# A macaron layer's setup: the FFN weight quantised on VectorE alone in a written order, the projection's weight and the attention bias prepared later, the second stack of values loaded three slots sooner

## The chip, the cores and the metric

The kernel runs on one core of one Trainium2 chip. The metric is the device time of one execution in microseconds, as the median of several runs. A profile of one execution shows what each engine did: TensorE (PE, and PEld for its weight loads), VectorE (DVE), ScalarE (ACT), GpSimd (POOL), and SyncE (SP), which issues nearly all DMAs.

## The reference

Input x is (4, 4096, 512) in float32: 16384 tokens of 512 features. The layer is half a feed-forward, a neighbourhood attention (16 heads of 32, 13 keys around each query, a relative bias per head), and the same half feed-forward again, each with a layer norm and a residual. The feed-forward quantises both its input and its weight in blocks of 32 to a 6-bit float grid.

```python
def _mx_quantize(t, eps=1e-30):
    blocks = t.reshape(rows, K // BLOCK_SIZE, BLOCK_SIZE)
    scales = jnp.maximum(jnp.max(jnp.abs(blocks), axis=-1) / FP6_E2M3_MAX, eps)
    q = _nearest_on_grid(blocks / scales[..., None], _GRID)
    return (q, scales)

def _L0_ffn_ref(x, weight, bias):
    xq, xs = _mx_quantize(x2);  wq, ws = _mx_quantize(w2)
    return (xq * xs[..., None]) @ (wq * ws[..., None]).T + bias

def _L0_attn_ref(x, qkv_w, qkv_b, rpb, proj_w, proj_b):
    qkv = x @ qkv_w.T + qkv_b
    attn = jnp.einsum('bhld,bhlkd->bhlk', q * SCALE, k[:, :, nbr, :]) + rpb[:, bidx][None]
    attn = jax.nn.softmax(attn, axis=-1)
    out = jnp.einsum('bhlk,bhlkd->bhld', attn, v[:, :, nbr, :])
    return out @ proj_w.T + proj_b

x = x + 0.5 * _L0_ffn_ref(_layernorm(x), ffn_weight, ffn_bias)
x = x + _L0_attn_ref(_layernorm(x), qkv_w, qkv_b, rpb, proj_w, proj_b)
x = x + 0.5 * _L0_ffn_ref(_layernorm(x), ffn_weight, ffn_bias)
```

## The kernel before

Every large product is made of float16 pairs: each operand is split into a high and a low half, and `product` (L146–154) runs 3 × 4 matmuls of 128 × 128 by 128 × 512. The halves are made by a ScalarE copy (`high`) and a VectorE subtraction followed by a DMA transpose on SyncE's queue (`low`). All five weight matrices lie transposed in one tile `wt`: query, key, value, projection (16 row chunks, numbered 0–3, 4–7, 8–11, 12–15) and FFN (16–19).

The work on the 128 token tiles is a pipeline written out by hand in slots. `begin(slot, stage, rank)` puts a generator into a slot, each `yield n, rank` moves its rest n slots on, and `run_slot` issues a slot's stages by rank. A tile t advances 7 slots behind tile t−1 (`STEP`). For a tile: load at 7t−18, moments (bn_stats) and the quantised norm from 7t−11 on (eight stages: factors on GpSimd, yq on ScalarE, block maxima on VectorE, a GpSimd product by 1/scale, the 8-bit rounding on ScalarE, a GpSimd product by the scale, high on ScalarE, low with the xT transpose), first feed-forward product (`pmf`) at 7t+5, second norm with the hln transpose at 7t+11, value product (`pmv`) at 7t+20. Four tiles form a group. For each of its four items of four heads (item m at 7m): Q/K products (`pmqk`) at +38, scores and softmax from +42 with the pT transpose at +52, the product with the values (`pv`) at +59. Output product (`pmo`) at 7t+93 and second feed-forward at 7t+105 end a tile.

The values go through DRAM (`vd`). `load_stack` (L394) reads them back as overlapping windows of keys, two stacks a group (head pairs 0–1 of items, and 2–3), three DMAs of about 357 KB each. The two stacks share a pool of two buffers (`vsp`). They are loaded at slots 28n+46 and 28n+56 for group n (L618–619).

The setup, from L622 on: the FFN weight `fw`, small inputs, tiles 0–2 and 16 row chunks `rows` are loaded. `junk` (L651) sums the squares of all rows on ScalarE; `powers` (L663) turns the largest into powers of two `up` and `down` by way of two small TensorE products. The FFN weight is then quantised in four chunks (L738–763): on VectorE the division, subtractions of `u`, a second division, the addition and the rounding to the grid (`tie_to_lower`); on GpSimd the two products `u` (L748) and the product back (L759); on ScalarE the 8-bit cast and the high half. Tiles 1 and 2 are normalised, and `scales`, `put_scaled` (high on ScalarE, low on VectorE, transpose into `wt`), `attention_bias` (the value bias taken through the projection, 12 matmuls `pmb`) and `put_table` (the relative bias, from the DMAs `rd`, `shifted`, `masks`) stand in slots 0 to 35.

What sets the order: up to `tc.manual_schedule()` at L772 the framework's scheduler orders the instructions of each engine by its own cost model; behind it, each engine runs them in the order in which the program issues them. So in this kernel the FFN weight, the first three norms and the DMAs ahead of L772 are ordered by the scheduler, and slots from −17 on as written.

```python
        begin(0, one(scales), 9)
        for slot, o in zip((2, 4, 5, 6, 10, 13, 16, 19, 21, 23, 25, 27, 29, 31, 33, 35), chunks):
            begin(slot, put_scaled(o), 9)
        begin(28, attention_bias(), 9)
```

Of the kernel before, what the change touches and what calls it, by code (L numbers as in the profile page):

```python
# [26 lines left out]
F32 = mybir.dt.float32  # L27
# [10 lines left out]
P = 128  # L38
# [26 lines left out]
def macaron_kernel(  # L65
# [96 lines left out]
    def begin(slot, stage, rank=5):  # L162
        slots.setdefault(slot, []).append((rank, stage))
# [402 lines left out]
    def one(f, *args):  # L566
        f(*args)
        return
        yield
# [45 lines left out]
    for n in range(n_batch * NG):  # L615
        k = n * GROUP * STEP
        b, g = divmod(n, NG)
        begin(k + 6 * STEP + 4, one(load_stack, b, g, 0), 9)  # L618
        begin(k + 8 * STEP, one(load_stack, b, g, 1), 9)


    with tc.tile_pool(name="setup", bufs=1) as sp, tc.tile_pool(name="scratch", bufs=2) as scr:  # L622
# [8 lines left out]
        nc.gpsimd.memset(rp, 0.0)  # L631
        nc.scalar.dma_start(out=rp[:, QR - 1 : QR - 1 + NREL], in_=rpb)


        rows = {}

        sq = sp.tile([P, 5 * KC], F32, name="sq")
        first = min(slots)
        for slot in range(first, first + EARLY * STEP, STEP):
            run_slot(slot)  # L640
        for _ in quantised_norms(-10):
            pass
        chunks = (8, 9, 10, 11, 12, 13, 14, 15, 0, 4, 1, 5, 2, 6, 3, 7)
        for o in chunks:
# [3 lines left out]
        for o in (*range(4 * KC, 5 * KC), *chunks):  # L648
# [3 lines left out]
        ptb = ps_m.tile([P, 512], F32, tag="mm", name="ptb")  # L652
        nc.tensor.transpose(ptb[:, : 3 * KC], b12, ident[: 3 * KC, : 3 * KC])
        bT = sp.tile([P, 3 * KC], F32, name="bT")
        nc.vector.tensor_copy(bT, ptb[:, : 3 * KC])
        b2 = sp.tile([P, 3 * KC], F32, name="b2")
        nc.vector.scalar_tensor_tensor(b2, bT, 2.0 ** -8, bT, ALU.mult, ALU.mult)
        nc.vector.tensor_tensor(sq[:, : 3 * KC], sq[:, : 3 * KC], b2, ALU.add)
        top5 = sp.tile([P, 5], F32, name="top5")
        up = sp.tile([P, 5], F32, name="up")  # L660
        down = sp.tile([P, 5], F32, name="down")

        def powers(lo, hi):  # L663

            w = hi - lo
            nc.vector.tensor_reduce(
                top5[:, lo:hi], sq[:, lo * KC : hi * KC].rearrange("p (m c) -> p m c", c=KC),
                AX.X, ALU.max,
            )
            ptn = ps_m.tile([P, 512], F32, tag="mm", name=f"ptn{lo}")  # L670
            nc.tensor.transpose(ptn[:w, :P], top5[:, lo:hi], ident)
            most = sp.tile([w, 1], F32, name=f"most{lo}")
# [3 lines left out]
            ones_w = sp.tile([w, P], F32, name=f"ones{lo}")  # L676
            nc.gpsimd.memset(ones_w, 1.0)
            pb = ps_m.tile([P, 512], F32, tag="mm", name=f"pb{lo}")
            nc.tensor.matmul(pb[:, :w], ones_w, diag, start=True, stop=True)
            e = sp.tile([P, w], I32, name=f"e{lo}")  # L680
# [11 lines left out]
        powers(4, 5)  # L692
        nc.vector.tensor_scalar(cf, down[:, 4:5], 0.5 / XS, None, ALU.mult)
        nc.gpsimd.tensor_scalar(half_ffn_b, half_ffn_b, 0.5, None, ALU.mult)

        def put_weights(o, hl):
            return nc.sync.dma_start_transpose(
# [19 lines left out]
        for o in range(KC):  # L717
            nc.vector.tensor_reduce(
                w_abs[:, o * NB : (o + 1) * NB], blocks(fw[:, o, :]), AX.X, ALU.max,
                apply_absolute_value=True,  # L720
            )
        nc.vector.tensor_scalar(w_sc, w_abs, 1.0 / Q_MAX, None, ALU.mult)
        split_scale()
        nc.vector.scalar_tensor_tensor(w_abs, w_hi, -Q_MAX, w_abs, ALU.mult, ALU.add)
        nc.vector.scalar_tensor_tensor(w_abs, w_lo, -Q_MAX, w_abs, ALU.mult, ALU.add)
        nc.vector.scalar_tensor_tensor(w_sc, w_abs, 1.0 / Q_MAX, w_sc, ALU.mult, ALU.add)
        nc.vector.tensor_scalar(w_sc, w_sc, Q_EPS, None, ALU.max)
        nc.vector.reciprocal(w_r, w_sc)
        split_scale()
        w_back = small("w_back")  # L730
        nc.vector.tensor_scalar(w_back, w_sc, up[:, 4:5], F8_SCALE, ALU.mult, ALU.mult)

        def large(name, o, dt=F32):
            return scr.tile(
                [P, NB, QB], dt, tag=name, bufs=3 if name == "wu_" else KC, name=f"{name}{o}"
            )

        for o in range(KC):  # L738
# [5 lines left out]
            qh, q0 = large("wqh_", o, F16), large("wq0_", o)  # L744
            nc.vector.tensor_tensor(qh, fwb, per(w_r), ALU.mult)
            for i, b in enumerate((w_hi, w_lo)):
                u = large("wu_", f"{o}_{i}")
                nc.gpsimd.tensor_tensor(u, qh, per(b), ALU.mult)  # L748
                nc.vector.tensor_tensor(fwb, fwb, u, ALU.subtract)  # L749
            nc.vector.tensor_tensor(q0, fwb, per(w_r), ALU.mult)  # L750
            nc.vector.tensor_tensor(q0, q0, qh, ALU.add)
# [12 lines left out]

        for t in range(1, EARLY):
            moments(t * STEP - 10, t, "n1")
            for _ in quantised_norms(t * STEP - 10):
                pass
# [14 lines left out]

        su, sd = up, down
        tab = sp.tile([P, 1], F32, name="tab")
        vb = sp.tile([P, KC], F32, name="vb")
# [18 lines left out]

        def attention_bias():

            vbx = sp.tile([P, 2, KC, P], F16, name="vbx")
            nc.scalar.copy(vbx[:, 0], bc(vb, P))
            nc.vector.tensor_tensor(vbx[:, 1], bc(vb, P), vbx[:, 0], ALU.subtract)  # L810
            yield 3, 9
# [100 lines left out]
```

## Time and profile before

| | |
|---|---|
| median of 3 runs | 2408.76 us (2407.12 to 2414.85) |
| the profiled execution's own time | 2401.24 us |
| its span, first to last instruction | 2399.4 us |
| granted TensorE clock, mean | 0.993 |
| TensorE / VectorE / GpSimd / ScalarE busy | 95% / 84% / 83% / 55% |
| DMA engines, SyncE's queue, share of time | 75.6% |
| first feed-forward product on TensorE | 58.72 us |
| first Q/K product | 106.72 us |

A line of a group or of the timeline reads: start and length in us, engine (a trailing q is its instruction queue, which issues DMAs), source line, operation, out<-in by the program's names, shapes and count, and in brackets how long the engine had been idle and what released it. A line of waits reads: who waited for whom, us in total, times, longest. A line of windows reads: stretch, its length, busy time of PE, PEld, DVE, ACT and POOL with counts, the granted clock, the DMA engines' share and GB/s.

### The profile page before, as it was taken

What the parts mean: (1) busy time and instruction counts of PE and PEld (TensorE: products, weight loads), DVE (VectorE), ACT (ScalarE), POOL (GpSimd) and SP (SyncE); (2) the same over time, 40 slices, a digit from 0 to 9 for tenths busy, and PEclk for the clock granted to TensorE, in tenths of its full rate; (3) what the DMA queues carried; (4) which work ended last, traced back from release to release, by engine and by line L of the source; (5) the groups of instructions that cost most, each with busy time, mean ns of one, the idle gap of its engine ahead of it and who ended that gap; (6) DMA issues with size and microseconds to landing.
All of it is one profiled execution on the core that took longest, in us unless ns stands there. A gap on an engine that the chain in (4) does not pass through costs nothing.

```text
span 2399.4 us, 82333 instructions
## 1 busy us (share of the span) xinstructions
PE 2278.8 (95%) x35539; PEld 1114.0 (46%) x35539; DVE 2015.3 (84%) x3588; ACT 1327.1 (55%) x2080; POOL 1989.0 (83%) x2012
## 2 busy tenths in 40 slices
PE   0799999999999999999999999999999999999987
PEld 0244444444444444444444444444444444444442
DVE  8789888888888888888888888888888888888775
ACT  4455555555555556555555555555555555555442
POOL 5578888888888888888888888888888888888677
PEclk9899999999999999999999999999999999999998
DMA  5788888787787877778867778777778887777753
GB/s 153 145 150 153 158 164 158 148 157 151 145 161 156 152 150 159 146 153 162 161 145 156 150 146 167 153 154 147 159 139 156 158 158 146 162 148 143 137 115 90
DMA packets 925700, 360.58 MB, mean 150 GB/s; under 512 B 718876, under 2 KB 889752, under 8 KB 925336
## 3 DMA queue, kind: packets, MB, share of 16 engines
q1 hardware_dynamic: 924992, 354.79, 75.6%
q8 instruction: 278, 4.55, 0.8%
q10 hardware_dynamic: 344, 0.53, 0.1%
q14 instruction: 86, 0.70, 0.1%
HBM read 110.15 MB, written 67.29 MB: 74 GB/s over the span
## 4 chain that ended last, share of the span: by engine, by line
PE 89%; DVE 4%; DMA 3%; issue 1%; POOL 1%; ACT 1%; SPq 0%; DVEq 0%; ACTq 0%; POOLq 0%
PE pmqk L151 27%; PE pmf L151 26%; PE pmo L151 14%; PE pmv L151 13%; PE ps L433 6%; PE pv L503 3%; DMA xT<-hlq 2%; DVE hlq L204 0%; DVE fw L749 0%; DMA x<-hln 0%; DVE qk L373 0%; DVE stn L180 0%; POOL x L564 0%; ACT ring L530 0%; DVE whl L779 0%
## 5 line engine op out<-in xcount | busy, mean ns | idle before, releaser
L151 PE MATMUL pmf<-wt,xT 128*128 128x512 f16 x3048 | 703.1, 381 | 17.8 <-DMA xT<-hlq 17.7
L151 PE MATMUL pmqk<-x,wt 128*128 128x512 f16 x3072 | 707.7, 380 | 6.2 <-DMA x<-hln 5.4
L151 PEld LDWEIGHTS <-xT 128*128 128x128 f16 x3048 | 297.0, 98 | 386.1 <-DMA xT<-hlq 29.3
L151 PEld LDWEIGHTS <-wt 128*128 128x128 f16 x3072 | 290.0, 98 | 343.1 <-issue 9.7
L151 PE MATMUL pmv<-wt,x 128*128 128x512 f16 x1536 | 353.8, 380 | 5.1 <-DMA x<-hln 5.1
L151 PE MATMUL pmo<-wt,ring 128*128 128x512 f16 x1536 | 355.3, 381 | 2.6 <-issue 2.6
L246 POOL TENSOR_TENSOR yq<-yq,r 128x1024 f32<-128x1024 f32 (+1 forms) x141 | 246.2, 1746 | 130.8 <-DVE r L244 130.8
L564 POOL TENSOR_TENSOR x<-x,half_ffn_b 128x512 f32<-128x512 f32 x256 | 327.4, 1279 | 0.1
L275 DVE SCALAR_TENSOR_TENSOR x<-pmf,coef,x 128x512 f32<-128x512 f32 x256 | 179.5, 701 | 165.2 <-PE pmf L151 164.7
L530 ACT ACTIVATE ring<-pv 128x510 f16<-128x510 f32 (+8 forms) x224 | 82.3, 414 | 400.5 <-PE pv L503 400.5
L310 ACT CAST vt<-pmv 128x512 f16<-128x512 f32 x128 | 74.9, 585 | 389.3 <-PE pmv L151 389.3
L180 DVE BATCH_NORM_STATS2 stn<-x 128x6 f32<-128x512 f32 x384 | 265.3, 691 | 8.9 <-DMA x<-in_L_attn_x_dram 0.2
L251 POOL TENSOR_TENSOR yq<-q,sc 128x1024 f32<-128x1024 fp8e4 (+1 forms) x141 | 246.7, 1749 | 0.4 <-ACT q L249 0.4
L151 PEld LDWEIGHTS <-x 128*128 128x128 f16 x1536 | 150.5, 98 | 187.6 <-DMA x<-hln 5.6
L373 DVE SCALAR_TENSOR_TENSOR qk<-pmqk,qk_b,qk 128x512 f16<-128x512 f32 x256 | 190.6, 744 | 53.8 <-ACT qk L369 53.0
L476 POOL TENSOR_TENSOR sf<-sf,total 128x714 f32<-128x714 f32 (+2 forms) x128 | 178.6, 1395 | 44.2 <-DVE total L474 25.0
L151 PEld LDWEIGHTS <-ring 128*128 128x128 f16 x1536 | 140.2, 98 | 161.5 <-issue 4.2
L186 POOL TENSOR_SCALAR rsq<-mv 128x2 f32<-128x2 f32 (+1 forms) x141 | 131.3, 931 | 96.0 <-DVE mv L181 93.8
L249 ACT ACTIVATE q<-yq,nudge 128x1024 fp8e4<-128x1024 f32 (+1 forms) x141 | 149.9, 1063 | 108.0 <-POOL yq L246 99.8
L369 ACT ACTIVATE qk<-pmqk,qk_b 128x512 f16<-128x512 f32 x256 | 176.1, 688 | 53.2 <-PE pmqk L151 52.1
L233 ACT ACTIVATE yq<-x,nbq,rsq 128x512 f32<-128x512 f32 x254 | 193.0, 804 | 20.8 <-POOL nbq L192 20.2
L467 POOL TENSOR_TENSOR sf<-sf,top 128x714 f32<-128x714 f32 (+2 forms) x128 | 180.4, 1409 | 20.0 <-DVE top L465 19.8
(145 smaller groups left out, 3466.9 us busy)
## 6 DMA issues: line engine op xcount, KB each, us to landing
vs<-vd SPq DMA_DIRECT2D x144, 357.0 KB
x<-in_L_attn_x_dram SPq DMA_DIRECT2D x128, 256.0 KB
vd<-vt SPq DMA_DIRECT2D x128, 256.0 KB
out_dram<-x SPq DMA_DIRECT2D x128, 256.0 KB
vs<-vd SPq DMA_DIRECT2D x24, 378.0 KB
vs<-vd SPq DMA_DIRECT2D x24, 315.0 KB
rows<-in_L_attn_qkv_w_dram SPq DMA_DIRECT2D x12, 256.0 KB
xT<-hlq SPq DMA_TRANSPOSE x141
```

What stands on the lines that cost most here:

```text
L151: nc.tensor.matmul(pm, lhs(a, c), rhs(b, c), start=(n == 0), stop=(n == 3 * KC - 1))
L180: nc.vector.bn_stats(st, xs[t])
L233: nc.scalar.activation(y[:, u], xs[t], AF.Identity, bias=nb[:, u : u + 1], scale=rs[:, u : u + 1])
L246: nc.gpsimd.tensor_tensor(yb, yb, bc(r, QB), ALU.mult)
L249: nc.scalar.activation(q8, y, AF.Identity, bias=nudge, saturate=False)
L251: nc.gpsimd.tensor_tensor(yb, q8.rearrange("p u (n q) -> p (u n) q", q=QB), bc(sc, QB), ALU.mult)
L275: nc.vector.scalar_tensor_tensor(xs[t], pm, cf, xs[t], ALU.mult, ALU.add)
L369: nc.scalar.activation(t[:, s, 0, KN:], pms[s], AF.Identity, bias=bias)
L373: nc.vector.scalar_tensor_tensor(t[:, s, 1, KN:], pms[s], bias, t[:, s, 0, KN:], ALU.add, ALU.subtract)
L467: nc.gpsimd.tensor_tensor(s, s, bc(top[:, :n], KN), ALU.subtract)
L476: nc.gpsimd.tensor_tensor(s, s, bc(total[:, :n], KN), ALU.mult)
L564: nc.gpsimd.tensor_tensor(xs[t], xs[t], b, ALU.add)
```

## The change

`manual_schedule` moves up to just behind the first loads, so that nearly the whole setup runs in the order in which it is written. The quantisation of an FFN chunk becomes a generator `quantise` with two yields, whose three GpSimd products run on VectorE; its steps are interleaved by hand with those of the first three norms and with the squares of the row chunks in fours. `half_ffn_b` is halved on ScalarE in place of GpSimd. `powers` and `scales` are cut into parts of one slot each. The squares now come in the order value, query and key, projection, with the projection's four last of all.

The projection's four chunks are squared early, dropped, loaded a second time at slots 61, 64, 68 and 71, and scaled five slots later, with their halves in tiles of the pool of x. The attention bias goes from slot 28 to 80. The query and key chunks take slots 13 to 35, the value chunks 3 to 6. The second stack of a group is loaded at 28n+53 in place of 28n+56.

```diff
-        begin(k + 8 * STEP, one(load_stack, b, g, 1), 9)
+        begin(k + 7 * STEP + 4, one(load_stack, b, g, 1), 9)
...
+        ctx.enter_context(tc.manual_schedule())
...
-        chunks = (8, 9, 10, 11, 12, 13, 14, 15, 0, 4, 1, 5, 2, 6, 3, 7)
+        chunks = (8, 9, 10, 11, 0, 4, 1, 5, 2, 6, 3, 7, 12, 13, 14, 15)
...
-        nc.gpsimd.tensor_scalar(half_ffn_b, half_ffn_b, 0.5, None, ALU.mult)
+        nc.scalar.activation(half_ffn_b, half_ffn_b, AF.Copy, scale=0.5)
...
+        ffn_power = powers(4, 5)
+        next(ffn_power)
...
+        next(ffn_power)
+        next(norms[0])
...
+        next(norms[0])
+        for _ in ffn_power:
+            pass
...
+        def quantise(o):
...
-            for i, b in enumerate((w_hi, w_lo)):
-                u = large("wu_", f"{o}_{i}")
-                nc.gpsimd.tensor_tensor(u, qh, per(b), ALU.mult)
+            for b in (w_hi, w_lo):
+                nc.vector.tensor_tensor(u, qh, per(b), ALU.mult)
                 nc.vector.tensor_tensor(fwb, fwb, u, ALU.subtract)
...
-            nc.gpsimd.tensor_tensor(fwb, w8, per(w_back), ALU.mult)
+            yield
+            nc.vector.tensor_tensor(fwb, w8, per(w_back), ALU.mult)
             hl = scr.tile([P, 2, dim], F16, tag="whl", bufs=4, name=f"whlf{o}")
             nc.scalar.copy(hl[:, 0, :], fw[:, o, :])
+            yield
             nc.vector.tensor_tensor(hl[:, 1, :], fw[:, o, :], hl[:, 0, :], ALU.subtract)
             put_weights(4 * KC + o, hl)
...
-        ctx.enter_context(tc.manual_schedule())
...
+        step(ready[3])
+        step(ready[2])
+        step(norms[1])
+        step(norms[2])
+        step(ready[3])
+        step(norms[1])
+        step(ready[3])
+        for _ in range(5):
+            step(norms[2])
+        for o in chunks[12:]:
+            square(o)
...
         def put_scaled(o):
             s = up[:, o // KC : o // KC + 1]
-            hl = scr.tile([P, 2, dim], F16, tag="whl", bufs=4, name=f"whl{o}")
+            if o < 3 * KC:
+                hl = scr.tile([P, 2, dim], F16, tag="whl", bufs=4, name=f"whl{o}")
+            else:
+                load_rows(o)
+                hl = xp.tile([P, dim], F32, tag="x", name=f"whl{o}").bitcast(F16)
+                hl = hl.rearrange("p (s k) -> p s k", s=2)
+                yield 5, 9
             nc.scalar.activation(hl[:, 0, :], rows[o], AF.Copy, scale=s)
...
-            powers(0, 4)
+            yield from powers(0, 4)
...
-        begin(0, one(scales), 9)
-        for slot, o in zip((2, 4, 5, 6, 10, 13, 16, 19, 21, 23, 25, 27, 29, 31, 33, 35), chunks):
+        begin(0, scales(), 9)
+        for slot, o in zip((3, 4, 5, 6, 13, 16, 20, 23, 26, 29, 32, 35, 61, 64, 68, 71), chunks):
             begin(slot, put_scaled(o), 9)
-        begin(28, attention_bias(), 9)
+        begin(80, attention_bias(), 9)
```

More of the change, by code (lines that the diff above doesn't have):

```diff
@@ L632, in macaron_kernel, with load_rows @@
         nc.scalar.dma_start(out=rp[:, QR - 1 : QR - 1 + NREL], in_=rpb)
+        ctx.enter_context(tc.manual_schedule())
         rows = {}
         sq = sp.tile([P, 5 * KC], F32, name="sq")
[L638 to L642, printed above, removed]
-        chunks = (8, 9, 10, 11, 12, 13, 14, 15, 0, 4, 1, 5, 2, 6, 3, 7)
-        for o in chunks:
+        chunks = (8, 9, 10, 11, 0, 4, 1, 5, 2, 6, 3, 7, 12, 13, 14, 15)
+        def load_rows(o):
             w, i = (qkv_w, o) if o < 3 * KC else (proj_w, o - 3 * KC)
@@ L647, in macaron_kernel, with square @@
             nc.sync.dma_start(out=rows[o], in_=w[i * P : (i + 1) * P, :])
-        for o in (*range(4 * KC, 5 * KC), *chunks):
+        def square(o):
             src = fw[:, o - 4 * KC, :] if o >= 4 * KC else rows[o]
@@ L651, in macaron_kernel @@
             nc.scalar.activation(junk, src, AF.Square, accum_out=sq[:, o : o + 1])
[L652 to L658, printed above, removed]
+        for o in range(4 * KC, 5 * KC):
+            square(o)
         top5 = sp.tile([P, 5], F32, name="top5")
-        up = sp.tile([P, 5], F32, name="up")
-        down = sp.tile([P, 5], F32, name="down")
+        up = const.tile([P, 5], F32, name="up")
+        down = const.tile([P, 5], F32, name="down")
         def powers(lo, hi):
@@ L671, in powers @@
             nc.tensor.transpose(ptn[:w, :P], top5[:, lo:hi], ident)
+            ones_w = sp.tile([w, P], F32, name=f"ones{lo}")
+            nc.gpsimd.memset(ones_w, 1.0)
+            yield 1, 9
             most = sp.tile([w, 1], F32, name=f"most{lo}")
@@ L675, in powers @@
             nc.vector.tensor_scalar(diag, ident[:w, :w], most, 2.0, ALU.mult, ALU.mult)
-            ones_w = sp.tile([w, P], F32, name=f"ones{lo}")
-            nc.gpsimd.memset(ones_w, 1.0)
             pb = ps_m.tile([P, 512], F32, tag="mm", name=f"pb{lo}")
             nc.tensor.matmul(pb[:, :w], ones_w, diag, start=True, stop=True)
+            yield 1, 9
             e = sp.tile([P, w], I32, name=f"e{lo}")
@@ L690, in powers @@
             nc.vector.tensor_scalar(d, d, 23, None, ALU.logical_shift_left)
-        powers(4, 5)
-        nc.vector.tensor_scalar(cf, down[:, 4:5], 0.5 / XS, None, ALU.mult)
-        nc.gpsimd.tensor_scalar(half_ffn_b, half_ffn_b, 0.5, None, ALU.mult)
         def put_weights(o, hl):
@@ L721, in macaron_kernel @@
             )
+        first = min(slots)
+        for slot in range(first, first + EARLY * STEP, STEP):
+            run_slot(slot)
+        for o in chunks:
+            load_rows(o)
+        ffn_power = powers(4, 5)
+        next(ffn_power)
+        nc.scalar.activation(half_ffn_b, half_ffn_b, AF.Copy, scale=0.5)
+        norms = {t: quantised_norms(t * STEP - 10) for t in range(EARLY)}
+        next(norms[0])
         nc.vector.tensor_scalar(w_sc, w_abs, 1.0 / Q_MAX, None, ALU.mult)
         split_scale()
+        next(ffn_power)
+        next(norms[0])
         nc.vector.scalar_tensor_tensor(w_abs, w_hi, -Q_MAX, w_abs, ALU.mult, ALU.add)
@@ L729, in macaron_kernel @@
         split_scale()
+        next(norms[0])
+        for _ in ffn_power:
+            pass
         w_back = small("w_back")
         nc.vector.tensor_scalar(w_back, w_sc, up[:, 4:5], F8_SCALE, ALU.mult, ALU.mult)
+        nc.vector.tensor_scalar(cf, down[:, 4:5], 0.5 / XS, None, ALU.mult)
         def large(name, o, dt=F32):
[L734 to L738, printed above, removed]
+            return scr.tile([P, NB, QB], dt, tag=name, name=f"{name}{o}")
+        def quantise(o):
             fwb = blocks(fw[:, o, :])
@@ L742, in per @@
                 return bc(t[:, o * NB : (o + 1) * NB], QB)
-            qh, q0 = large("wqh_", o, F16), large("wq0_", o)
+            qh, q0, u = large("wqh_", o, F16), large("wq0_", o), large("wu_", o)
             nc.vector.tensor_tensor(qh, fwb, per(w_r), ALU.mult)
-            for i, b in enumerate((w_hi, w_lo)):
-                u = large("wu_", f"{o}_{i}")
-                nc.gpsimd.tensor_tensor(u, qh, per(b), ALU.mult)
+            for b in (w_hi, w_lo):
+                nc.vector.tensor_tensor(u, qh, per(b), ALU.mult)
                 nc.vector.tensor_tensor(fwb, fwb, u, ALU.subtract)
@@ L758, in macaron_kernel @@
             )
-            nc.gpsimd.tensor_tensor(fwb, w8, per(w_back), ALU.mult)
+            yield
+            nc.vector.tensor_tensor(fwb, w8, per(w_back), ALU.mult)
             hl = scr.tile([P, 2, dim], F16, tag="whl", bufs=4, name=f"whlf{o}")
             nc.scalar.copy(hl[:, 0, :], fw[:, o, :])
+            yield
             nc.vector.tensor_tensor(hl[:, 1, :], fw[:, o, :], hl[:, 0, :], ALU.subtract)
             put_weights(4 * KC + o, hl)
[L765 to L768, printed above, removed]
@@ L772, in macaron_kernel, with step @@
-        ctx.enter_context(tc.manual_schedule())
+        ready = [quantise(o) for o in range(KC)]
+        def step(g):
+            next(g, None)
+        step(ready[0])
+        step(norms[0])
+        step(norms[0])
+        for o in chunks[:4]:
+            square(o)
+        moments(STEP - 10, 1, "n1")
+        step(ready[0])
+        step(norms[0])
+        step(ready[1])
+        step(ready[0])
+        step(norms[0])
+        step(norms[1])
+        step(norms[1])
+        moments(2 * STEP - 10, 2, "n1")
@@ new lines, in macaron_kernel @@
+        step(ready[1])
+        step(norms[0])
+        for o in chunks[4:8]:
+            square(o)
+        step(ready[2])
+        step(ready[1])
+        step(norms[1])
+        step(norms[1])
+        step(norms[1])
+        step(norms[2])
+        step(norms[2])
+        step(ready[2])
+        step(norms[1])
+        for o in chunks[8:12]:
+            square(o)
+        step(ready[3])
+        step(ready[2])
+        step(norms[1])
+        step(norms[2])
+        step(ready[3])
+        step(norms[1])
@@ new lines, in macaron_kernel @@
+        step(ready[3])
+        for _ in range(5):
+            step(norms[2])
+        for o in chunks[12:]:
+            square(o)
+        ptb = ps_m.tile([P, 512], F32, tag="mm", name="ptb")
+        nc.tensor.transpose(ptb[:, : 3 * KC], b12, ident[: 3 * KC, : 3 * KC])
+        bT = sp.tile([P, 3 * KC], F32, name="bT")
+        nc.vector.tensor_copy(bT, ptb[:, : 3 * KC])
+        b2 = sp.tile([P, 3 * KC], F32, name="b2")
+        nc.vector.scalar_tensor_tensor(b2, bT, 2.0 ** -8, bT, ALU.mult, ALU.mult)
@@ L774, in put_scaled @@
+        nc.vector.tensor_tensor(sq[:, : 3 * KC], sq[:, : 3 * KC], b2, ALU.add)
         def put_scaled(o):
             s = up[:, o // KC : o // KC + 1]
-            hl = scr.tile([P, 2, dim], F16, tag="whl", bufs=4, name=f"whl{o}")
+            if o < 3 * KC:
+                hl = scr.tile([P, 2, dim], F16, tag="whl", bufs=4, name=f"whl{o}")
+            else:
+                load_rows(o)
+                hl = xp.tile([P, dim], F32, tag="x", name=f"whl{o}").bitcast(F16)
+                hl = hl.rearrange("p (s k) -> p s k", s=2)
+                yield 5, 9
@@ L785, in macaron_kernel @@
         tab = sp.tile([P, 1], F32, name="tab")
-        vb = sp.tile([P, KC], F32, name="vb")
+        vb = const.tile([P, KC], F32, name="vb")
         def scales():
-            powers(0, 4)
+            yield from powers(0, 4)
             nc.vector.tensor_scalar(cp, sd[:, 2:3], sd[:, 3:4], 1.0 / XS, ALU.mult, ALU.mult)
@@ L806, in attention_bias @@
         def attention_bias():
-            vbx = sp.tile([P, 2, KC, P], F16, name="vbx")
+            vbx = xp.tile([P, dim], F32, tag="x", name="vbx").bitcast(F16)
+            vbx = vbx.rearrange("p (s c q) -> p s c q", s=2, c=KC)
             nc.scalar.copy(vbx[:, 0], bc(vb, P))
```

## The prediction

> **What bounds the kernel now.** I read the page first, then TensorE's waits, the busy time by windows, and the timeline of the start and of two DMA stretches. Page and windows:
>
> ```profile
> span 2399.4 us, 82333 instructions
> PE 2278.8 (95%) x35539; PEld 1114.0 (46%) x35539; DVE 2015.3 (84%) x3588; ACT 1327.1 (55%) x2080; POOL 1989.0 (83%) x2012
> ...
> 20.00:40.00 20.00, 0.38 (x1) 0.08 (x1) 20.00 (x31) 7.25 (x20) 15.81 (x13) 1.00 0.20 59
> ...
> 80.00:100.00 20.00, 11.78 (x37) 4.29 (x38) 18.23 (x34) 10.84 (x17) 10.08 (x16) 0.67 0.83 168
> ...
> 300.00:400.00 100.00, 100.00 (x1510) 48.97 (x1508) 87.07 (x154) 57.47 (x90) 86.86 (x85) 1.00 0.83 161
> ```
>
> A window row gives TensorE, its weight loads, VectorE, ScalarE and GpSimd, then clock, DMA share and GB/s. From about 107 us on TensorE is the bound (100 of 100 us). Of its 121 us idle, 73 lie before 107 us and some 18 in the waits of the tail after 2330. In the start VectorE is the bound: full at 20–40, 18.23 of 20 at 80–100. Only three things can win time: the start, waits of TensorE in the middle, and the tail, which the change leaves alone.
>
> The start, from the timeline: the weight products of GpSimd and VectorE in alternation, the first feed-forward product, the attention-bias product, the first Q/K product.
>
> ```profile
> 28.09 1.49 POOL L748 TENSOR_TENSOR wu<-wqh,w_lo 128x512 f32<-128x512 f16 x1
> 28.60 1.53 DVE L751 TENSOR_TENSOR wq<-wq,wqh 128x512 f32<-128x512 f32 x1
> 29.55 1.49 POOL L748 TENSOR_TENSOR wu<-wqh,w_hi 128x512 f32<-128x512 f16 x1
> 30.05 1.53 DVE L750 TENSOR_TENSOR wq<-fw,w_r 128x512 f32<-128x512 f32 x1
> ...
> 58.72 4.79 PE L151 MATMUL pmf<-wt,xT-10_160 128*128 128x512 f16 x12 [15.19 <-DMA wt<-whlf]
> ...
> 96.28 3.59 PE L151 MATMUL pmb<-wt,vbx 128*128 128x512 f16 x8 [3.67 <-DVE vbx L810]
> ...
> 106.72 5.34 PE L151 MATMUL pmqk<-x,wt 128*128 128x512 f16 x24 [1.33 <-DMA x<-hln]
> ```
>
> Each pair of one GpSimd and one VectorE product advances 1.45 us (28.60 to 30.05). Without GpSimd VectorE starts one every 0.60 (45.28, 45.88, 46.48 in the chain). So one GpSimd product costs VectorE 0.85 us.
>
> TensorE's waits between 300 and 2300 us, and the DMA queue around 480 and 146 us:
>
> ```profile
> PE pmf L151 <- DMA xT<-hlq: 7.1, 9, 1.6
> ...
> 473.69 1.58 SPq L409 DMA_DIRECT2D vs<-vd  x3
> 475.36 2.10 SPq L555 DMA_DIRECT2D out_dram<-x  x1
> 477.51 0.43 SPq L176 DMA_DIRECT2D x<-in_L_attn_x_dram  x1
> 479.02 5.29 SPq L485 DMA_TRANSPOSE pT<-p  x1
> 484.40 3.12 SPq L205 DMA_TRANSPOSE xT<-hlq  x1
> ...
> 142.26 3.73 SPq L409 DMA_DIRECT2D vs<-vd  x6
> 146.61 5.78 SPq L485 DMA_TRANSPOSE pT<-p  x1
> 153.83 1.30 SPq L205 DMA_TRANSPOSE x<-hln  x1
> 158.15 4.44 PE L151 MATMUL pmqk<-x,wt 128*128 128x512 f16 x12 [4.11 <-DMA x<-hln]
> ```
>
> The second stack load goes out just ahead of the pT transpose; pT then holds SyncE's queue 5.29 us (2.4 behind a first load, at 532.12), and xT behind it is late. The nine waits recur at one phase of the 70 us group.
>
> **The change, part by part.**
>
> *FFN weight on VectorE alone.* Before, four chunks take 8 VectorE operations each (0.60 apiece, the bit-or 0.34: 4.54, so 18.2 us), with norms, scales and small work about 25 us, and 18 GpSimd products of chunks and norms cost 18 × 0.85 = 15.3. That gives 40.5 from 15.4, so 55.9; the trace has the last VectorE step of the weight end at 55.0, so the account holds. After: 11 operations a chunk (6.34 × 4 = 25.4), two statistics 1.55, two block maxima 1.7, two low halves 1.2, and only five norm products of GpSimd in the way (4.3): 34.2 us. The e, up and down operations of the FFN power now stand ahead, so it begins at about 16.7 instead of 15.4, and ends at 50.9. [...] The new VectorE form, a product out of 8-bit values, has no row; the 0.60 of the other forms and GpSimd's contended 1.45 bound it: 0 to 3.4 us for four. I take 0.60, since GpSimd itself needs 1.04 for that form and 1.05 for float.
>
> *What is late next.* The xT transposes share one hlq buffer, so the third tile's high half waits for the second's transpose: issued about 50.4, 3.25 to land (as 55.38 to 58.63), so 53.7. Only behind that do ScalarE's last four squares run (4 × 0.62, to 57), then the maximum, transpose, diagonal and spread of the other powers (2.4 us; the FFN's took 3.0, 9.47 to 12.51, with other VectorE work between). These two small products stand ahead of the first feed-forward product on TensorE, which thus starts at 59.4 although its weights landed at about 55: 0.7 us late, bounds −4 and +4.
>
> *SyncE in the start.* The table's DMAs (rd, then shifted, masks; issue 0.68 + 1.77 + 2.45) and x3's load lay at 17.9–28.8; they now stand behind xT of tile 2 (about 55.2) and ahead of V's four transposes (1.29 each). shifted waits for rd: 6.0 us from issue in a full queue (17.86 to 23.89), 3.2 for a transpose in a free one; I take 3.2, the queue being free at 50–54 (share 0). So: xT issued by 56.5, rd landed 59.7, shifted and masks out by 64, x3 by 64.5, 3 to land (3.9 in a full queue, 5.91 to 9.81). x3 lands near 67.5 and its statistics start at 67.5 instead of 66.34: +1.2 (0 to +4). GpSimd's six mask selects (1.37) fall in its idle time; half_ffn_b's 1.51 on GpSimd becomes one ScalarE copy (0.7) beside idle time.
>
> *Projection's parts and bias out of slots 10–35.* Ahead of the fourth hln, which starts the first Q/K product, three VectorE low parts of 0.74 and vbx 0.68 go (2.9 us; 3.5 with one 1.24 contended), ScalarE loses the same number, SyncE 3 × 1.29. I take 3.5 (0 to 7: VectorE is full at 80–100, latency-bound before). TensorE's pmb leaves its 4.6 at half clock, off the path but for 0.2. First Q/K product: +1.2 − 3.5 = **−2.3 us** (−7 to +4).
>
> *The same, late.* Slots 61–77: four 256 KB loads again, four ScalarE parts (0.72), four VectorE (0.74), four transposes; vbx and after_b 0.62 + 0.68 + 0.74. At 160–180 us VectorE is busy 14.67 of 20 and the DMA share 0.55: they fit; at 180–200 VectorE has 18.55 and DMA 1.01. **+0.5** (0 to 4). pmb on the bound engine, 12 matmuls at 0.216: **+2.6**.
>
> *Second stack three slots sooner.* It now follows xT and hln, as the first load does (517.58, 519.58, 521.52). Its buffer's last reader is the pv product one slot earlier, which TensorE ends about 4 us before SyncE gets there (499.5 against 503.8): no wait. The DMA engines are idle at 470–474, so the load uses that and pT finds a freer queue; xT was at most 1.6 us late and gains about 3. **−7.1** (0 to −7.1). In the early case the DMA share at 142–146 is 0.43 and 0.56, about 2 us idle; the 4.11 wait falls by **−2** (0 to −4.1). The matmuls after it run 4.44 instead of 2.70, with a granted clock of 0.57 in 158–162; behind waits of 2.13 and 2.41 (1740, 2313) matmuls stay at full pace, so **−1.7** (0 to −1.7). [...]
>
> Sum: −2.3 + 0.5 + 2.6 − 7.1 − 2.0 − 1.7 = **−10.0 us**. The profiled execution took 2401.24 us (span 2399.4), so 2391.2; the median of the runs shown, 2408.76, lies 7.5 above it, so **2398.8**.
>
> **Rivals.**
>
> *The start wins its four microseconds too.* If the squares and the power chain run before the last norm, the first product starts at about 55: 4.4 less, **2394**. For it: TensorE has nothing else there. Against: one ScalarE queue in written order. Chance 0.15.
>
> *The stack load only moves its collision.* xT stays late by as much: without the −7.1 the sum is −2.9, **2406**. For it: DMA shares of 1.0–1.2 around both loads. Against: no xT wait follows a first load. Chance 0.22.
>
> *Slower: two loads in consecutive steps.* The first goes out at slot 46 and the second now at 53, seven slots apart instead of ten; a step with a load fills about 17 of 17.6 us of DMA (share near 1 from 516 to 532 and 534 to 540). If the backlog adds up, the xT after it is late in nearly all 30 groups; at the mean of the present waits, 0.78 us, that costs 23: −2.9 + 23, **2429**. It decides from a third of a microsecond a group. Against: behind a first load xT goes out at 535.16, needs 5.2 (484.40 to 489.61), and its product starts at 542.38, 2 us to spare. Chance 0.15.
>
> **How the numbers follow.** Forecast 0.48, rivals 0.15, 0.22, 0.15. About 0.3% (7.2 us) is what a measurement of this kernel can tell from no change. The forecast's own range, from the bounds of the start above all, is 2391 to 2405, some three quarters of it below 2401.5; with the first rival: faster 0.52. Within: a fifth of the forecast and most of the second rival, 0.32. Slower: the third rival and a sliver, 0.16. The range 2387 to 2413 leaves out most of the third rival and the far end of the start.
>
> **What would show it.** First feed-forward product at 59 ± 3 with weights landed earlier; the powers' small products just ahead of it; the first Q/K product near 104; pmb about 2.6 us long at full clock in the steady part; no xT waits between 300 and 2300, pT after second loads near 2.5–3 us; the wait before the fifth Q/K item about 2. Wrong it would be if xT waits recur elsewhere in the group, if VectorE's start ends after 55, or if Q/K start past 110.

## The result, and the profile after

The changed kernel takes 2441.35 us (median of 6 runs, 2438.58 to 2451.1); the kernel before, run beside it, 2410.43 us (6 runs, 2407.12 to 2418.08). The ratio is 1.0125, 95% interval 1.0110 to 1.0141: it is slower by about 31 us, where 10 us less had been forecast. The profiled execution took 2439.54 us.

The page of the changed kernel (busy time by engine, the granted clock in 40 slices, SyncE's DMA queue and TensorE's instruction queue, one group of instructions):

```profile
span 2437.8 us, 82350 instructions
...
PE 2290.6 (94%) x35539; PEld 1117.7 (46%) x35539; DVE 2013.5 (83%) x3600; ACT 1330.1 (55%) x2081; POOL 1976.9 (81%) x1999
...
PEclk9899999999999999999999999999999999999998
...
q1 hardware_dynamic: 925568, 355.84, 78.5%
q8 instruction: 278, 4.55, 0.8%
...
L151 PE MATMUL pmo<-wt,ring 128*128 128x512 f16 x1536 | 362.6, 386 | 18.4 <-issue 18.3
```

TensorE does the same 35539 matmuls in a span 38.4 us longer. VectorE and GpSimd have no more work than before. But the packets of SyncE's queue take 78.5% of the DMA engines' time, against 75.6% of a shorter span, for 0.3% more bytes (354.79 to 355.84 MB), and the output product now stands idle 18.3 us, named "issue": time in which the engine waited for nothing that the profile shows.

The steady window of the prediction again (length, busy PE, PEld, DVE, ACT, POOL, clock, DMA share, GB/s), and one behind a late restart:

```profile
300.00:400.00 100.00, 100.00 (x1575) 49.13 (x1573) 85.89 (x153) 58.61 (x91) 87.02 (x85) 1.00 0.81 155
1995.00:2007.00 12.00, 7.24 (x96) 3.10 (x95) 6.40 (x10) 2.28 (x5) 5.67 (x5) 0.86 0.73 131
```

The quiet 100 us are as full as before. The loss sits in single places such as the last row: TensorE works 7.24 of 12 us, at a clock of 0.86.

The start, by the timeline: three VectorE products in a row on the way to the weight (each reads what the one before wrote or writes over what it read), the powers' small products and the first feed-forward product, the attention-bias product, the first Q/K product.

```profile
16.39 0.69 DVE L755 TENSOR_TENSOR wu<-wqh,w_hi 128x512 f32<-128x512 f16 x1
17.12 0.69 DVE L756 TENSOR_TENSOR fw<-fw,wu 128x512 f32<-128x512 f32 x1
17.84 0.69 DVE L755 TENSOR_TENSOR wu<-wqh,w_lo 128x512 f32<-128x512 f16 x1
...
59.19 0.38 PE L666 MATMUL ptn<-ident,top 128*4 128x128 f32 x1 [47.11 <-DVE top L661]
60.28 0.56 PE L675 MATMUL pb<-diag,ones 4*128 4x4 f32 x2 [0.71 <-DVE diag L673]
60.77 4.50 PE L151 MATMUL pmf<-wt,xT-10_308 128*128 128x512 f16 x12
...
106.39 6.00 PE L151 MATMUL pmqk<-x,wt 128*128 128x512 f16 x14 [5.35 <-DMA x<-hln]
...
199.89 2.75 PE L151 MATMUL pmb<-wt,vbx 128*128 128x512 f16 x12 [0.74 <-DVE stn L180]
```

The first Q/K product begins 0.3 us earlier than before, but behind a wait of 5.35 us and at half clock (the trace grants 0.50 from 105.27 to 112.10): its first 14 matmuls alone take 6.00 us where 24 took 5.34. The start ends about 2.5 us later than before.

TensorE's waits between 300 and 2300 us (who waited for whom, us in total, times, longest): the issue waits of the kernel before, then all of the changed kernel, then SyncE's queue around 480 us and one of the new waits:

```profile
PE ps L433 <- issue: 3.1, 3, 1.5
PE pmo L151 <- issue: 2.6, 2, 2.1
PE pv L503 <- issue: 1.3, 3, 0.7
PE pmqk L151 <- issue: 0.8, 2, 0.5
```

```profile
PE pmo L151 <- issue: 9.2, 3, 4.8
PE ps L433 <- issue: 8.8, 6, 3.0
PE pmqk L151 <- issue: 4.8, 4, 2.5
PE pv L503 <- issue: 3.9, 7, 1.3
PE pmqk L151 <- DVE mv L181: 3.0, 1, 3.0
```

```profile
480.46 1.64 SPq L409 DMA_DIRECT2D vs<-vd  x3
...
490.46 3.12 SPq L485 DMA_TRANSPOSE pT<-p  x1
493.67 3.00 SPq L205 DMA_TRANSPOSE xT<-hlq  x1
...
1987.89 1.66 SPq L409 DMA_DIRECT2D vs<-vd  x3
1997.74 3.44 SPq L485 DMA_TRANSPOSE pT<-p  x1
...
1994.29 0.82 PE L151 MATMUL pmo<-wt,ring 128*128 128x512 f16 x3
1999.87 3.67 PE L151 MATMUL pmo<-wt,ring 128*128 128x512 f16 x9 [4.76 <-issue]
```

The waits for xT (7.1 us before) are gone, and pT behind a second load takes 3.12 us in place of 5.29, close to the forecast of 2.5 to 3. In their place "issue" waits have grown from 7.8 us in this stretch to 26.7. In the last two lines TensorE stops in the middle of one product, three matmuls in, with nine to go whose operands are the same tiles. The packet records of the trace show what arrives there. Queue q8 above, named "instruction", moved 278 blocks of 16 KB, 4.55 MB in all; by division that is 64 bytes for each of some 71 thousand matmuls and weight loads, and the blocks are taken here for TensorE's program. One of them ran from 1996.49 to 1998.38; TensorE went on 1.5 us later. The issue waits look alike from 300 us on: a 16 KB packet ends 1.2 to 1.8 us before the restart, and a stack load `vs<-vd` was issued 7 to 13 us before it. So the block of instructions is late. That it is queued behind the load's packets is the reading that the experiments put to the test.

Behind six of these waits, of 2.98 to 4.76 us, the trace grants a clock of 0.50 for 3.41 us each. The two shortest of the six are 2.98 us (before 616.11) and 3.01 (before 1781.25). A wait of 2.46 us at 1764.9 was not followed by it. In the experiments below one of 1.97 us was (late load, clock 0.57 from 1446 to 1450) and one of 3.26 us was not (sooner load alone, 1.00 from 1965 to 1974), so the length of a wait alone does not decide it in these traces.

The 38.4 us of the two spans then read: late instruction blocks +29.8 (13.8 to 43.6 us over the whole span, the 3.0 us that the profile puts down to VectorE's `mv` among them, since that wait too ends behind such a packet), half clock behind six of them +10.2 (6 × 1.7, half of 3.41 each), xT −7.1, the attention-bias product with its wait +3.3, the start +2.5, one wait at 221 +1.4, the two waits for pT in the tail −2.2: 37.9.

### The profile page after: what moved, and what is told of

Same layout as the page of the kernel before. It is cut to its first block, busy times and chain, and to the rows that moved or that the text cites. A ratio compares the mean times of both kernels' runs of the same rounds, so it can differ in the third digit from the quotient of the medians.

```text
span 2437.8 us, 82350 instructions
## 1 busy us (share of the span) xinstructions
PE 2290.6 (94%) x35539; PEld 1117.7 (46%) x35539; DVE 2013.5 (83%) x3600; ACT 1330.1 (55%) x2081; POOL 1976.9 (81%) x1999
## 3 DMA queue, kind: packets, MB, share of 16 engines
q1 hardware_dynamic: 925568, 355.84, 78.5%
q8 instruction: 278, 4.55, 0.8%
## 4 chain that ended last, share of the span: by engine, by line
PE 89%; DVE 5%; issue 2%; DMA 2%; POOL 1%; ACT 1%; SPq 0%; ACTq 0%; DVEq 0%; POOLq 0%
PE pmqk L151 27%; PE pmf L151 26%; PE pmo L151 13%; PE pmv L151 13%; PE ps L433 6%; PE pv L503 3%; DMA x<-hln 1%; DVE stn L180 1%; DMA xT<-hlq 1%; DVE hlq L204 1%; POOL x L564 0%; DVE sc L239 0%; POOL yq L246 0%; DVE wu L755 0%; DVE fw L756 0%
## 5 line engine op out<-in xcount | busy, mean ns | idle before, releaser
L151 PE MATMUL pmf<-wt,xT 128*128 128x512 f16 x3048 | 704.0, 381 | 11.5 <-DMA xT<-hlq 11.4
L151 PE MATMUL pmo<-wt,ring 128*128 128x512 f16 x1536 | 362.6, 386 | 18.4 <-issue 18.3
L373 DVE SCALAR_TENSOR_TENSOR qk<-pmqk,qk_b,qk 128x512 f16<-128x512 f32 x256 | 190.7, 745 | 73.9 <-ACT qk L369 73.4
```

The costliest lines, as they stand in the source:

```text
L151: nc.tensor.matmul(pm, lhs(a, c), rhs(b, c), start=(n == 0), stop=(n == 3 * KC - 1))
L373: nc.vector.scalar_tensor_tensor(t[:, s, 1, KN:], pms[s], bias, t[:, s, 0, KN:], ALU.add, ALU.subtract)
```

## The experiments

**First four: is it the sooner load, the start, or the burst?** Theory A had the sooner load make the instruction blocks late; rival B blamed the start and the late parts.

*The changed kernel with the second load at its old place.*

```diff
-        begin(k + 7 * STEP + 4, one(load_stack, b, g, 1), 9)
+        begin(k + 8 * STEP, one(load_stack, b, g, 1), 9)
```

> The changed kernel with the second stack put back to slot 28n+56; all else as changed. Theory A (the earlier load makes TensorE's instruction blocks arrive late: in the trace of the changed kernel the waits that end about 1.3 us after a block's packet sum to 43 us against 14 before, and the half-clock stretches behind the long ones cost 10 more): about 2441 - 30 - 10 + 7 (the xT waits return) + 2 = 2410, 2405 to 2420. Rival B (projection parts and bias late, or the new start, do the harm; the load only saved 7): 2445 to 2450.

Measured: 2466.61 us, ratio to before 1.0242 (1.0216 to 1.0268). Its waits, 300 to 2300 us:

```profile
PE pmf L151 <- DMA xT<-hlq: 20.3, 17, 2.6
PE pv L503 <- issue: 13.7, 9, 3.7
PE pmqk L151 <- issue: 9.2, 6, 2.9
PE pmo L151 <- issue: 5.8, 2, 3.0
PE ps L433 <- issue: 1.7, 1, 1.7
```

Without the sooner load it is 25 us slower still: the load is a gain in the changed kernel too. And xT waits 20.3 us in place of 7.1, though load and xT stand in the slots of before. The issue waits, 30.4 us in all, are no fewer than the 26.7 with the sooner load. Theory A falls; rival B's 2445 to 2450 was too low as well.

*The kernel before with the sooner load alone.*

```diff
-        begin(k + 8 * STEP, one(load_stack, b, g, 1), 9)
+        begin(k + 7 * STEP + 4, one(load_stack, b, g, 1), 9)
```

> The kernel before with one edit: the second stack at slot 28n+53. Theory A: 2410 + 30 + 10 - 7 = about 2440, 2428 to 2448. Rival B: 2410 - 7 = 2403, 2399 to 2408, with no xT waits in the steady part and TensorE's waits on its instructions as before.

Measured: 2399.76 us, ratio 0.9952 (0.9934 to 0.9969), about −11.5 us. Its only waits between 300 and 2300:

```profile
PE pmo L151 <- issue: 9.0, 5, 3.3
PE ps L433 <- issue: 6.0, 3, 4.3
```

The load alone gives what was forecast for it, with xT waits gone and issue waits up from 7.8 to 15.0. The trace also has three stretches of half clock between 300 and 2300 us (6.83 us from 824.75, 3.41 each from 1026.13 and 1541.55) where the kernel before has none.

*The changed kernel with the projection's parts and the bias early again* (slots 10 to 18 and 28, parts in their own tiles of `scr`).

```diff
-        for slot, o in zip((3, 4, 5, 6, 13, 16, 20, 23, 26, 29, 32, 35, 61, 64, 68, 71), chunks):
+        for slot, o in zip((3, 4, 5, 6, 13, 16, 20, 23, 26, 29, 32, 35, 10, 12, 15, 18), chunks):
...
-        begin(80, attention_bias(), 9)
+        begin(28, attention_bias(), 9)
```

> The changed kernel with the projection's parts at slots 10, 12, 15, 18 and the bias at 28, so nothing of the setup is late; start order and earlier second load kept. Theory A: the load's harm stays; pmb's 2.6 and about 2 of late waits go, the first Q/K product comes 2 to 4 later: 2436 to 2444. Rival B with the late parts at fault: 2403 to 2415.

Measured: 2442.65 us, ratio 1.0121 (1.0098 to 1.0144). The late parts have no share in the loss that this could tell from noise.

*The changed kernel with the three DMAs of each stack two slots apart* (the `yield` stands in `load_stack`, behind each of the three).

```diff
+            yield 2, 9
...
-        begin(k + 6 * STEP + 4, one(load_stack, b, g, 0), 9)
-        begin(k + 7 * STEP + 4, one(load_stack, b, g, 1), 9)
+        begin(k + 6 * STEP + 4, load_stack(b, g, 0), 9)
+        begin(k + 7 * STEP + 4, load_stack(b, g, 1), 9)
```

> The changed kernel with the three DMAs of each stack two slots apart (46, 48, 50 and 53, 55, 57) in place of one slot. Theory A in the form that a burst of one megabyte is what an instruction block queues behind: a third of the burst, so waits on instructions fall below 15 us, 2400 to 2415. If only the sum of DMA work in the two steps counts: 2435 to 2445.

Measured: 2402.82 us, ratio 0.9971 (0.9956 to 0.9986). Waits, 300 to 2300, with the queue's share of the DMA engines:

```profile
q1 hardware_dynamic: 925568, 355.84, 79.8%
```

```profile
PE ps L434 <- issue: 5.5, 5, 1.7
PE pmo L151 <- issue: 3.8, 3, 1.6
```

The share is the highest of all, 79.8%, yet the issue waits fall from 26.7 to 9.3 us, at the same addresses and for the same bytes. So the waits go with how much is queued at once, not with the share. Spreading also makes the loads' own 512-byte packets shorter: a median of 35 ns and a mean of 47 between 300 and 2300 us, against 47 and 51 in the changed kernel.

**What was left.** The load gains in both kernels and the late parts cost nothing, and still the changed setup loses 40 us to the kernel before with the same load (2441 and 2400). The packet records showed a difference nobody had written: a 512-byte packet of the stack loads took, between 300 and 2300 us, a median of 39 ns (mean 43 or 44) before and with the sooner load alone, but 46 or 47 ns (mean 50 or 51) in the changed kernel and with its late load or early parts. The code of the loads is the same. The addresses of the built program are not:

```diff
-        up = sp.tile([P, 5], F32, name="up")
-        down = sp.tile([P, 5], F32, name="down")
+        up = const.tile([P, 5], F32, name="up")
+        down = const.tile([P, 5], F32, name="down")
...
-        vb = sp.tile([P, KC], F32, name="vb")
+        vb = const.tile([P, KC], F32, name="vb")
```

The late parts still need these three small tiles, so the change takes them out of the setup's pool into `const`. Each occupies 32 bytes a partition, and every pool opened after `const` moves up by 96. The two stack buffers begin at 204288 and 213504 before, both multiples of 256; in the changed kernel at 204384 and 213600, both 96 above one. That is theory C. Rival D keeps the loss in the start's order.

**Second four: the addresses.** The first two edits are one unused tile at the end of `const`.

*The changed kernel, moved on to the next multiple of 256.*

```diff
     halo = const.tile([P, KC, 2, 2, KN], F16, name="halo")
+    pad = const.tile([P, 40], F32, name="pad")
+    nc.vector.memset(pad, 0.0)
```

> The changed kernel with an unused tile of 160 bytes a partition at the end of the pool const. The change moves up, down and vb (32 bytes each with their padding) into const, so that every pool opened later lies 96 bytes higher: the stack buffers vs at 204384, 96 above a multiple of 256; with the unused tile at 204544, a multiple of 256 again (before: 204288). Theory C (the addresses: packets of 512 bytes into the stack took a median 47 ns after and 39 before, so each stack load keeps the queues longer and TensorE's instruction blocks come late): the waits named issue fall from some 40 us to those of the run with the sooner load alone (about 20 in all), packets at 39 ns, and the time is 2395 to 2405. Rival D (the addresses are harmless, and the loss comes from the order of the start or what it leaves in the queues): 2441 as after.

Measured: 2398.58 us, ratio 0.9965 (0.9948 to 0.9982); packets at 39 ns. Page and waits (300 to 2300):

```profile
q1 hardware_dynamic: 925568, 355.84, 73.9%
```

```profile
PE pmo L153 <- issue: 8.4, 4, 3.8
PE ps L435 <- issue: 6.1, 5, 3.3
PE pmqk L153 <- issue: 0.6, 2, 0.4
```

160 unused bytes turn 1.0125 into 0.9965, and the queue's share falls from 78.5% to 73.9% for the same 925568 packets and 355.84 MB.

*The kernel before, moved by 96 bytes and not otherwise changed.*

```diff
     halo = const.tile([P, KC, 2, 2, KN], F16, name="halo")
+    pad = const.tile([P, 24], F32, name="pad")
+    nc.vector.memset(pad, 0.0)
```

> The kernel before with an unused tile of 96 bytes at the end of const, and nothing else: every later pool lies 96 bytes higher, as in the changed kernel. Theory C: packets of 512 bytes at 46 to 47 ns instead of 39, waits for xT and for instruction blocks grow as in the run of the changed kernel with the late load (2467); 2440 to 2466. Rival D: 2410, as before.

Measured: 2451.36 us, ratio 1.0200 (1.0178 to 1.0222); packets at 47 ns.

```profile
q1 hardware_dynamic: 924992, 354.79, 78.7%
```

```profile
PE pmf L153 <- DMA xT<-hlq: 19.1, 18, 2.5
PE pmqk L153 <- issue: 9.0, 7, 2.6
PE pv L505 <- issue: 7.3, 9, 1.6
PE pmo L153 <- issue: 6.4, 2, 3.3
PE ps L435 <- issue: 1.9, 1, 1.9
```

The shift alone costs the kernel before 2.0%, with the pattern of the late-load run: xT late twice as often, issue waits up from 7.8 to 24.6 us. Rival D falls.

*The changed kernel with only the stack buffers moved back.*

```diff
+    padp = ctx.enter_context(tc.tile_pool(name="padp", bufs=1))
+    pad = padp.tile([P, 40], F32, name="pad")
+    nc.vector.memset(pad, 0.0)
     vsp = ctx.enter_context(tc.tile_pool(name="vsp", bufs=2))
```

> The changed kernel with the unused 160 bytes in a pool of their own just ahead of the stack buffers: these alone lie at a multiple of 256 again (204544); x, the transposed norms, Q/K, P and pT stay 96 bytes higher than before. Theory C with the stack loads as the cause: as the run with all pools moved back, 2395 to 2405. If the other transfers' buffers (x, halves transposed, Q/K) share in it: between, 2410 to 2430. Rival D: 2441.

Measured: 2401.02 us, ratio 0.9987 (0.9974 to 1.0000); packets at 39 ns, the queue at 75.2%. Nearly all of the loss is the stack buffers'. What the other pools add, 0.9987 against 0.9965, is within what the two intervals leave open.

*Both mends: loads two slots apart, and the 160 bytes.*

> The changed kernel with each stack's three loads two slots apart (2403 by itself, at the shifted addresses) and the unused 160 bytes in const. Theory C: both shorten the backlog in front of an instruction block; the 9 us of issue waits left with the spread loads go mostly, 2388 to 2400. Rival D: 2403, as without the 160 bytes.

Measured: 2387.52 us, ratio 0.9930 (0.9911 to 0.9948), half a microsecond under the expected range. Of the 9.3 us of issue waits 5.9 are left, so they did not go mostly; there is one wait for xT of 1.6 us. The 512-byte packets took a median of 27 ns (mean 39), against 39 (44) with the 160 bytes alone.

**Last four: the terms of the sum, the best version, and which boundary.**

*The changed kernel with the late load and the 160 bytes*: only start, parts and bias are left of the change.

> The changed kernel with the second load back at its place of before and the unused 160 bytes in const: start, parts and bias of the change alone, at the addresses of before. Theory C: it differs from before by the recorded start and late parts alone; the profiles gave the start +2.5 and the parts +3, so 2406 to 2414 beside 2406 to 2410 for before, waits for xT of about 7 between 300 and 2300 as before. Rival D (something in the start costs more): over 2425.

Measured: 2409.16 us, ratio 1.0008 (0.9990 to 1.0026). The start, the parts and the bias together are worth +2 us, with an interval of −2 to +6. The xT waits of before are back (300 to 2300), and the issue waits sum to 8.1 us, as the 7.8 of before:

```profile
PE pmf L153 <- DMA xT<-hlq: 4.8, 9, 0.9
```

*The kernel before with both load changes* (sooner, and two slots apart; the two edits shown above, at the addresses of before).

> The kernel before with the second load three slots sooner and each stack's three loads two slots apart, at the addresses of before. Theory C: the two gains add as they do in the changed kernel (2399 to 2388); from 2400 with the sooner load alone to 2384 to 2392, at or a little under the changed kernel with both (2388), since its start is 2 to 3 shorter. If the spread loads help only behind the changed start: 2396 to 2402.

Measured: 2377.89 us, ratio 0.9881 (0.9852 to 0.9909): better than expected, and the fastest of all.

```profile
PE pmo L151 <- issue: 4.9, 4, 1.7
PE ps L434 <- issue: 3.0, 3, 2.1
PE pmf L151 <- DMA xT<-hlq: 0.7, 1, 0.7
```

No wait reaches 2.2 us between 300 and 2300, and no stretch of half clock is left there. Why it lies 0.5% below the changed kernel with the same loads, where the start's +2 us explain 0.1%, stays open; the intervals of the two ratios (0.9911 to 0.9948 and 0.9852 to 0.9909) nearly touch.

*The stack buffers 128 and 64 above a multiple of 256* (8 and 56 floats in the pool `padp`, in the changed kernel).

> The changed kernel with 32 unused bytes just ahead of the stack buffers, which then begin 128 above a multiple of 256 (204416). It tells which boundary counts. If a packet is cut at multiples of 256 and its lead-in costs too, 512 bytes at 96 cost 608/512 of an aligned packet (39 ns make 46, measured 47), and at 128 they cost 640/512: 49 ns, and the time is that of after or a little over, 2440 to 2452. If a multiple of 64 or 128 is enough: 39 ns and 2400.

> The same with 224 unused bytes: the stack buffers begin 64 above a multiple of 256 (204608). Cut at multiples of 256 with the lead-in paid: 576/512 of 39 ns, 44 ns, and 2420 to 2440. If a multiple of 64 is enough: 39 ns and 2400.

Measured: at 128, 2421.33 us, ratio 1.0074 (1.0042 to 1.0106); at 64, 2436.12 us, 1.0127 (1.0093 to 1.0161). The packets took a median of 45 ns in both (mean 48 and 49), against 39 (44) on a multiple of 256 and 47 (51) at 96. The 45 ns at 128 and its time miss what was expected for it (49 ns, 2440 to 2452); those at 64 lie near it. So a multiple of 64 or 128 is not enough: of the offsets tried, only the multiple of 256 has 39 ns. What the two expectations suppose of a cause is not shown by any run. Their fractions of 39 ns make 44 at 64, 46 at 96 and 49 at 128; measured were 45, 47 and 45. So they fit at 64 and 96, but not in the order: 128 was no dearer than 64. The time at 128 lies below that at 64 although the packets differ by hardly a nanosecond; these runs don't tell why.

## Why the prediction was wrong

**The step that failed is one that the sum has no term for.** It counted what instructions cost on the engines and in SyncE's queue, and took every transfer that the change leaves alone at its duration of before ("a step with a load fills about 17 of 17.6 us of DMA"). That three small tiles change their pool was costed at nothing without being named, under "only three things can win time: the start, waits of TensorE in the middle, and the tail". It cost the changed kernel 1.0125 against 0.9965, 1.6% or 39 us. With the 160 bytes that undo it, the change measures 0.9965, −8 us (−13 to −4), beside a forecast of −10.

The mechanism in numbers: a packet of 512 bytes takes 7 ns more, and there are 123 thousand of them between 300 and 2300 us, so each of the 16 DMA engines is busy some 54 us longer by this estimate. A higher share need not cost time (the spread loads have the highest, 79.8%, at 2402.82 us), but the packets come in bursts of a megabyte just ahead of other work. In the kernel before, xT and TensorE's instruction blocks are both late behind them, by the waits: with the shift alone the waits for xT grow from 7.1 to 19.1 us and the issue waits from 7.8 to 24.6. With the sooner load xT is out of the way, and the instruction blocks alone are late: 26.7 us and the 3.0 named `mv`, against 15.1 with the 160 bytes.

**The sooner load: right in size, and in the waits for xT.** Forecast −7.1, −2.0 and −1.7, together −10.8; measured 0.9952 alone (−11.5) and, at equal addresses, 0.9965 against 1.0008 in the changed kernel (−10). The waits for xT went as forecast. The −2.0 and −1.7 at the fifth Q/K item did not show in the changed kernel (3.97 us, half clock), but with the addresses mended the timeline has

```profile
155.83 2.75 PE L153 MATMUL pmqk<-x,wt 128*128 128x512 f16 x12 [0.92 <-DMA x<-hln]
```

in place of 4.11 us of wait and 4.44 of length: −3.2 and −1.7. What the forecast left out is that the gain is partly given back: issue waits grew from 7.8 to 15 us, and with the load alone three stretches of half clock cost 6.8 us more. In the two profiled executions this takes back the whole gain (2401.24 us before, 2401.77 with the load alone); the one before happened to lie 7.5 us under the median of its runs. The gain of 10 to 11 us is a difference of medians, and the waits of these profiles do not add up to it. That it meets the −10.8 so closely may be luck.

**The start: wrong sign, small.** Forecast −2.3 at the first Q/K product, measured −0.3 there and +2.8 more through half clock behind a wait of 5.35 us. Part of this too goes with the addresses: the second Q/K product starts at 118.32 before and at 120.80 in the changed kernel, but with the 160 bytes at 119.16, or 119.48 with the late load. That still leaves about +1 where −2.3 was forecast. VectorE ended the weight at 53.15 (52.47 + 0.68), not 50.9, though it began it at 15.68, a microsecond sooner than forecast. The term that was mis-sized is 0.60 for each product: products that depend on the one before them start every 0.73 us (16.39, 17.12, 17.84), eight in a chunk, which makes 4 us in four chunks; the 0.60 came from rows in which the scheduler had put independent operations side by side. Two such operations start 0.60 apart in the changed kernel too (30.08 and 30.68). SyncE's part of the start moved with it: xT of tile 2 was issued at 57.60 (forecast 55.2), and the issue of x3 ended at 68.10 (67.52 + 0.58; forecast 64.5). The other steps hold: the powers' small products do stand just ahead of the first feed-forward product (59.19 and 60.28, then 60.77; forecast 59.4), `rd` and the table's DMAs follow xT of tile 2.

**The late parts: right within a microsecond.** pmb took 2.75 us at full clock (forecast 2.6) behind a wait of 0.74; of the rest, forecast at 0.5, no wait between 160 and 300 us gives a sign once the 160 bytes are in.

**The rivals.** "Two loads in consecutive steps" was on the right side (2429 for 2441) with the wrong mechanism. It needed xT late in nearly all 30 groups; in the changed kernel xT has no wait at all between 300 and 2300 us, and the late load is 25 us slower at the same addresses. "The stack load only moves its collision" had something of the truth, since at the addresses of before the 7 us of waits for xT made way for 7 us more of issue waits, but by the medians the gain of 10 to 11 us stands there.

## What to carry to other kernels

A tile that changes its pool moves every pool opened later. Before costing a change, compare the buffers' addresses, and keep those that many small DMA packets write on a multiple of 256 bytes: in these runs a 512-byte packet took a median of 39 ns there, and 45 to 47 at 64, 96 and 128 above it. When an engine's waits are named "issue" and begin in the middle of a product, look in the packet records for its instruction blocks (here one ended 1.2 to 1.8 us before each restart) and at which large transfer was issued some 10 us earlier (here a stack load, 7 to 13 us), and spread that transfer out (here 26.7 us of issue waits became 9.3).

## What the runs showed of the hardware that was not expected

- A shift of 96 bytes in all buffers behind `const` took the 512-byte packets of the stack loads from a median of 39 to 47 ns, and an otherwise unchanged kernel from 2406 to 2451 us. Moving the stack buffers alone back undoes nearly all of it.
- What is taken here for TensorE's program comes by DMA, on the queue named "instruction", in blocks of 16 KB that take 0.9 to 1.9 us each. In the changed kernel the waits that end behind one sum to 43.6 us over the span, and behind six of them, of 2.98 to 4.76 us, the granted clock was 0.50 for 3.41 us each.
- Spreading each stack's three loads over slots two apart is worth 0.7% beside the sooner load in the kernel before (0.9952 to 0.9881) and 1.5% in the changed kernel (1.0125 to 0.9971), although it raises the queue's share of the DMA engines there (78.5% to 79.8%). At the changed kernel's mended addresses it is worth 0.35% (0.9965 to 0.9930), and the 512-byte packets fall from a median of 39 to 27 ns with it.
